# A fused Perceiver layer on one core: masks added to pairs of PSUM banks, the first key projection moved ahead of the scores, context loaded piece by piece

## The chip, the cores and the metric

The kernel runs on one core of a Trainium2 chip. The metric is the device time of one execution in microseconds (us), taken as the median of several runs. The engines named below are PE (matrix products), DVE and POOL (elementwise work), ACT (activations and copies), and SP, which here only issues DMA transfers. [...] Each engine works through its own instructions in the order in which they were written; engines meet through semaphores.

## The reference

The input is `x` (32 batches of 64 rows of 256) and a context of 1601 rows of 256 for each batch. Three blocks with residual connections follow each other. Cut to what matters here, the first is

```python
qh, kh, vh = split_heads(q @ wq + bq), split_heads(ctx @ wk + bk), split_heads(ctx @ wv + bv)
scores = einsum('bhqd,bhkd->bhqk', qh, kh) / sqrt(16)        # 16 heads of 16
attn   = softmax(where(mask, scores, -1e9), axis=-1)         # over 1601 keys
x      = x + merge(attn @ vh) @ wo + bo                      # q = layernorm(x)
```

The second block is attention over the 64 positions of a batch whose weights come from a learned mean and width for each position and head. The third is a feed-forward layer: a shared gated part and two of eight experts for each token, chosen by the token's number. All is float32.

## The kernel before, in words

The 1601 keys of a batch are padded to 13 blocks of 124. The context arrives transposed in four pieces for each batch (`GROUPS`: 4, 3, 3 and 3 blocks) through five buffers `ct` (`load_piece`, `load_context`). For each batch `project_keys(b, c, g)` makes the keys of one half `c` of the heads (eight heads) and one group `g`, and ACT copies them from PSUM to `kT` (L510). `project_values(b, u)` makes the values of two blocks and ACT copies them to `v` (L527). A projection is either one product over the whole array or "tiled", four products of 32 columns each (L495).

The attention of a half (b, c) is computed with keys on the partitions. `scores(n, g)` computes the blocks of one of three score groups (`SCORED`: 4, 5 and 4 blocks) for four pairs of heads, one pair to a bank; the fifth block of the middle group goes to an extra bank and to spare room beside the accumulators `pvs`. DVE adds the mask `madd` to each bank and writes the result to `prob` in SBUF (L573, for the fifth blocks L566), and keeps a running maximum over the blocks in `mrun` (L590). In what order DVE does this is written out by hand in the strings `ORDER`, `SOONER` and `LATER`: a digit is the mask of one bank, `m7` the maximum over block 7, `t` the maximum along rows, A and B the fifth blocks. PE turns the maxima (`pm`, L597), DVE reduces them along rows (L604), PE spreads them again (`pb`, L612), ACT copies them to `mb` (L616), POOL subtracts them from `prob` (L621), ACT takes the exponential (L626), and PE multiplies with the values (`pvs`, L636).

The main loop runs over 63 halves, n = 0 to 62. In the turn of half n the scores of half n+1 are computed, the softmax of half n is finished, the values of half n-1 are multiplied, and the next batch is projected. In a turn of before, PE's order is: values of n-1, place 0; first scores of n+1; `pm`; keys of group 0; `pb`; values of n-1, place 1; second scores; keys of group 1; two value projections; third scores; keys of groups 2 and 3, tiled; one or two value projections, tiled. Between them stand the steps of the second block for earlier tiles of 128 rows and of the queries for later ones (`span_steps`, `query_steps`), handed out by `agenda`: for a tile these are eleven products into PSUM (`tr_q`, `pq`, `po`, `tr_h`, `psp`, `pval`, `psa` twice, `po2`, `po3`, `tr_f`). The order on PE, DVE, ACT and POOL is the order of the program (`manual_schedule`).

The PSUM banks for all of this except `pvs` and `mrun` come from one pool of six tiles, `ps_x`, handed out in turn by `mm_bank`. Waits between engines are derived from the tiles that the instructions touch. Towards the end, units of the feed-forward layer (`unit`, `gate`, `linear_factor`) use the same six banks; the experts follow with pools of their own.

Of the kernel before, what the change touches and what calls it, by code (L numbers as in the profile page):

```python
# [23 lines left out]
P = 128  # L24
# [14 lines left out]
ORDER = [  # L39
    "0 1 t 2 3",  # L40
    "A 0 m3 1 B 2 m8 3 m4 m5",
    "0 1 m6 2 m7 3 m9 m10 m11 m12",
]
# [24 lines left out]

SOONER = "A 0 1 B 2 m8 3 m4 m5"
LATER = "A 0 m1 1 m2 B 2 m3 3 m8 m4 m5"  # L70

# [19 lines left out]
def perceiver_kernel(ctx: ExitStack, tc: tile.TileContext, a: dict[str, bass.AP], out: bass.AP):  # L91
# [9 lines left out]
    span_pool = ctx.enter_context(tc.tile_pool(name="span", bufs=1))  # L101
    ps_mm = None

# [3 lines left out]

    def mm_bank(name: str):
        return ps_mm.tile([P, 512], F32, tag="mm", name=name)

# [134 lines left out]
    def span_steps(t: int, oT):  # L245
# [148 lines left out]

    ps_x = xattn.enter_context(tc.tile_pool(name="ps_x", bufs=6, space=PSUM))
    ps_pv = xattn.enter_context(tc.tile_pool(name="ps_pv", bufs=1, space=PSUM))
    ps_m = xattn.enter_context(tc.tile_pool(name="ps_m", bufs=1, space=PSUM))
    ps_mm = ps_x


    madd = big.tile([P, NKC, S], F32, name="madd", bufs=1)
    nc.vector.tensor_scalar(madd[:CHUNK], m8[:CHUNK], -MASKED, MASKED, ALU.mult, ALU.add)
    nc.vector.tensor_scalar(
        madd[:CHUNK, NKC - 1, :], madd[:CHUNK, NKC - 1, :], cst[:CHUNK, C_PAD : C_PAD + 1],
        None, ALU.add,
    )

    madd_fifth = big.tile([P, P], F32, name="madd_fifth", bufs=1)
    for e in range(2):
        nc.gpsimd.tensor_copy(  # L410
            madd_fifth[:CHUNK, e * S : (e + 1) * S], madd[:CHUNK, SCORED[1][0] + 4, :]
        )

# [4 lines left out]
    def pair_of(n: int, j: int):  # L421
        return prob[:CHUNK, place(n, j // 2), j % 2]
# [59 lines left out]

    def load_context(b: int):
        for g in range(len(GROUPS)):
            load_piece(b, g)
        if b % 2 == 0 and b // 2 + 1 < NTILE:
            t = b // 2 + 1
            load_x(t)

# [42 lines left out]
    def scores(n: int, g: int, then=None, order=None):  # L532
# [5 lines left out]
        more = [mm_bank(f"psc_{b}_{c}_{g}"), spare_pvs] if nb == 5 else None  # L538
        pss = [mm_bank(f"psc_{b}_{c}_{g}_{j}") for j in range(4)]
        for r in range(nb):  # L540
# [17 lines left out]
        for item in (order or ORDER[g]).split():  # L558
            if item == "t":
                if held is not None:  # L560
                    maxima_of_rows(*held)
            elif item[0] == "m":
                maximum(n, int(item[1:]))
            elif item in "AB":
                k, e = c0 + 4, "AB".index(item)
                nc.vector.tensor_tensor(  # L566
                    block_of(n, k)[:, :, e, :],
                    more[e][:CHUNK, : 2 * P].rearrange("p (r q) -> p r q", r=2),
                    madd_fifth[:CHUNK, None, :].to_broadcast([CHUNK, 2, P]), ALU.add,
                )  # L570
            else:
                j = int(item)
                nc.vector.tensor_tensor(  # L573
                    pair_of(n, j)[:, c0 : c0 + 4, :].rearrange("p k (e q) -> p k e q", e=2),
                    pss[j][:CHUNK].rearrange("p (k e q) -> p k e q", k=4, e=2),
                    madd[:CHUNK, c0 : c0 + 4, None, :].to_broadcast([CHUNK, 4, 2, S]), ALU.add,
                )
# [81 lines left out]

    def half_unit(u: int, w):  # L660
        quarter, hc = divmod(u, NHC)
        slot = slice(quarter * QL, (quarter + 1) * QL)
        ps = mm_bank(f"u{u}")
        for c in range(2):
            nc.tensor.matmul(  # L665
                ps, lhsT=w[:, c, hc * P : (hc + 1) * P], rhs=xfT[:, c, :, slot],
                start=(c == 0), stop=(c == 1),
            )
        return ps.rearrange("p (r i) -> p r i", r=E)
# [8 lines left out]
    def unit(u: int):  # L678
        begun.append((u, half_unit(u, sw1), None if u in linear else half_unit(u, sw3)))

    def gate():
        u, p1, p3 = begun.popleft()
        quarter, hc = divmod(u, NHC)
        at = gated_at(quarter, hc)
# [77 lines left out]
    for u in range(7):  # L762
        project_values(0, u)
    last = len(halves) - 1

    extra = {3 * last - 3: (0,), 3 * last - 2: (1, 2, 4), 3 * last - 1: (5, 6)}
    for n, (b, c) in enumerate(halves[:-1]):
        if c == 0 and b + 1 < B:
            load_context(b + 1)
        if c and b % 2 == 0 and b // 2 + 1 < NTILE:  # L770
# [16 lines left out]
        if n:  # L787
            values(n - 1, 0)
            exponentials(n - 1, 3)
        scores(n + 1, 0, taken_off)  # L790
        project(project_keys, c, 0)
        m = maxima_along_rows(turned[1])
# [18 lines left out]
        exponentials(n, 0)  # L811
        project(project_keys, c, 1)
        for u in (4, 5) if c else (0, 1):
            project(project_values, u)
        less_maxima(n, 1, m, nc.gpsimd)
# [4 lines left out]
        scores(n + 1, 2)  # L820
        project(project_keys, c, 2, True)
        project(project_keys, c, 3, True)
        for u in (3, 6) if c else (2,):
            project(project_values, u, True)
# [179 lines left out]
```

## Time and profile before

| | before |
|---|---|
| median of 3 runs | 1520.34 us (1519.32 to 1524.4) |
| span of the profiled execution | 1515.7 us; its own time is not given apart, the runs lie 3.6 to 8.7 us above its span |
| granted PE clock, mean | 0.995 |
| PE busy | 1465.0 us, 97% |
| DVE busy | 1225.5 us, 81% |
| POOL busy | 1120.7 us, 74% |
| ACT busy | 946.9 us, 62% |

A group's row in the profile names the line, the engine, the operation, what it writes and reads with shapes and the number of instructions; then its busy time, the mean duration of one in ns, and the idle time of the engine just before such instructions with what ended most of it. Busy shares are means over the span. PE's ends are modelled, so that groups that follow each other overlap a little in the timeline.

### The profile page before, as it was taken

What the parts mean: (1) busy time and instruction counts of PE and PEld (TensorE: products, weight loads), DVE (VectorE), ACT (ScalarE), POOL (GpSimd) and SP (SyncE); (2) the same over time, 40 slices, a digit from 0 to 9 for tenths busy, and PEclk for the clock granted to TensorE, in tenths of its full rate; (3) what the DMA queues carried; (4) which work ended last, traced back from release to release, by engine and by line L of the source; (5) the groups of instructions that cost most, each with busy time, mean ns of one, the idle gap of its engine ahead of it and who ended that gap; (6) DMA issues with size and microseconds to landing.
All of it is one profiled execution on the core that took longest, in us unless ns stands there. A gap on an engine that the chain in (4) does not pass through costs nothing.

```text
span 1515.7 us, 62949 instructions
## 1 busy us (share of the span) xinstructions
PE 1465.0 (97%) x28600; PEld 1066.5 (70%) x28600; DVE 1225.5 (81%) x2332; ACT 946.9 (62%) x1727; POOL 1120.7 (74%) x508
## 2 busy tenths in 40 slices
PE   8999999999999999999999999999999999998899
PEld 5677767777777767777777777676777677654587
DVE  4889898998989898989989898988899898873100
ACT  3565657676767657576766677575767566766411
POOL 1777787888878887878888888878788788852710
PEclk9999999999999999999999999999999999999999
DMA  5111111111111101111111111011111111005200
GB/s 174 37 45 46 46 47 46 36 50 50 50 50 50 49 25 41 47 53 37 49 50 50 50 50 49 24 43 46 54 37 48 50 50 33 3 9 160 60 29 29
DMA packets 52076, 73.82 MB, mean 49 GB/s; under 512 B 3812, under 2 KB 51040, under 8 KB 51680
## 3 DMA queue, kind: packets, MB, share of 16 engines
q1 hardware_dynamic: 50992, 69.00, 14.9%
q8 instruction: 225, 3.69, 1.0%
q10 hardware_dynamic: 816, 0.79, 0.2%
q14 instruction: 43, 0.35, 0.1%
HBM read 65.57 MB, written 4.19 MB: 46 GB/s over the span
## 4 chain that ended last, share of the span: by engine, by line
PE 76%; DVE 17%; ACT 4%; issue 2%; POOL 0%; DMA 0%; ACTq 0%; DVEq 0%; POOLq 0%
PE pk L495 20%; PE pv L495 19%; PE psc L549 10%; PE pvs L636 10%; DVE mrun L590 8%; DVE prob L573 6%; PE py L934 4%; PE pm L597 2%; PE u L665 2%; PE ph L916 2%; PE pb L612 2%; ACT qbd L474 1%; PE psa L357 1%; PE pq L466 1%; PE po L377 1%
## 5 line engine op out<-in xcount | busy, mean ns | idle before, releaser
L621 POOL TENSOR_TENSOR prob<-prob,mb 124x1664 f32<-124x1664 f32 x252 | 939.0, 3751 | 224.2 <-ACT mb L616 218.8
L573 DVE TENSOR_TENSOR prob<-psc,madd 124x512 f32<-124x512 f32 x768 | 504.0, 680 | 76.5 <-PE psc L549 76.0
L626 ACT ACTIVATE prob<-prob 124x1664 f32<-124x1664 f32 x256 | 406.9, 1591 | 185.0 <-POOL prob L621 182.0
L590 DVE TENSOR_TENSOR mrun<-prob,mrun 124x512 f32<-124x512 f32 x704 | 486.7, 691 | 33.9 <-ACT mrun L582 20.1
L495 PE MATMUL pk<-ct,wkT_sb 128*32 128x372 f32 (+1 forms) x2512 | 387.6, 489 | 8.9 <-DMA wkT_sb<-in_wkT 5.5
L495 PE MATMUL pv<-wvT_sb,ct 128*124 128x256 f32 x3524 | 381.0, 379 | 0.9 <-DVE prob L566 0.8
L495 PEld LDWEIGHTS pv<-wvT_sb,ct 128*124 128x124 f32 x3524 | 272.8, 132 | 110.4 <-issue 17.5
L549 PE MATMUL psc<-qbd,kT 32*124 32x128 f32 x6400 | 241.8, 279 | 8.3 <-issue 6.9
L495 PEld LDWEIGHTS pk<-ct,wkT_sb 128*32 128x32 f32 (+1 forms) x2512 | 148.9, 127 | 140.1 <-issue 95.5
L549 PEld LDWEIGHTS psc<-qbd,kT 32*124 32x124 f32 x6400 | 201.9, 181 | 41.8 <-issue 20.8
L636 PE MATMUL pvs<-prob,v 124*17 124x64 f32 x13312 | 213.6, 220 | 3.0 <-issue 2.8
L527 ACT COPY v<-pv 124x512 f32<-124x512 f32 (+1 forms) x224 | 124.5, 556 | 146.5 <-PE pv L495 146.1
L636 PEld LDWEIGHTS pvs<-prob,v 124*17 124x17 f32 x13312 | 196.0, 98 | 27.9 <-issue 15.7
L510 ACT ACTIVATE kT<-pk,cols 128x372 f32<-128x372 f32 (+2 forms) x256 | 145.7, 585 | 70.0 <-PE pk L495 69.7
L323 ACT ACTIVATE sc<-sc,least 128x64 f32<-128x64 f32 x256 | 85.8, 343 | 2.6 <-DVE least L319 2.5
L936 DVE SCALAR_TENSOR_TENSOR ot<-py,prob 128x256 f32<-128x256 f32 x16 | 6.8, 424 | 75.7 <-PE py L934 66.1
L665 PE MATMUL u<-xfT,sw_sb 128*128 128x512 f32 x128 | 60.9, 624 | 3.6 <-ACT prob L692 2.7
L582 ACT COPY mrun<-prob 124x512 f32<-124x512 f32 x64 | 38.2, 596 | 37.3 <-DVE soft L306 34.3
L612 PEld LDWEIGHTS pb<-cst,mc 128*124 128x124 f32 x256 | 29.4, 135 | 36.6 <-DVE mc L604 30.0
L549 PE MATMUL pvs<-qbd,kT 32*124 32x128 f32 x256 | 54.9, 294 | 0.0
L597 PE MATMUL pm<-cst,mx 124*128 124x124 f32 x256 | 41.4, 283 | 11.4 <-DVE mx L590 10.1
L323 ACT ACTIVATION_READ_ACCUMULATOR sc<-sc,least 128x1 f32 x256 | 49.9, 195 | 0.0
(126 smaller groups left out, 1220.3 us busy)
## 6 DMA issues: line engine op xcount, KB each, us to landing
ct<-in_ctxT SPq DMA_DIRECT2D x64, 372.0 KB, 3.2
ct<-in_ctxT SPq DMA_DIRECT2D x32, 496.0 KB, 5.1
ct<-in_ctxT SPq DMA_DIRECT2D x32, 361.0 KB, 3.9
w<-in_w SPq DMA_DIRECT2D x16, 256.0 KB, 7.0
x<-in_x SPq DMA_DIRECT2D x16, 128.0 KB, 2.1
x_kept<-x SPq DMA_DIRECT2D x16, 128.0 KB, 2.0
prob<-x_kept SPq DMA_DIRECT2D x8, 256.0 KB, 6.3
out<-ot SPq DMA_DIRECT2D x16, 128.0 KB, 1.9
```

Source lines behind the costliest of these rows:

```text
L323: nc.scalar.activation(sc[:, h, :], sc[:, h, :], AF.Exp, bias=least[:, h : h + 1], scale=-1.0, accum_out=total[:, h : h + 1],)
L495: nc.tensor.matmul(out[at:end], lhsT=lhsT[:, at:end], rhs=rhs, start=start, stop=stop, **(dict(tile_position=(0, at)) if tiled else {}),)
L510: nc.scalar.activation(kTs[c][:, k0 : k0 + kn], ps[:, :kn], AF.Identity, bias=cols[:, B_K + c : B_K + c + 1])
L527: nc.scalar.copy(vs[b % 2][:kn, 2 * u : 2 * u + n, :, :DK], ps[:kn, : n * D].rearrange("p (n h d) -> p n h d", n=n, d=DK),)
L549: product = nc.tensor.matmul(ps[:CHUNK, at * P : (at + 1) * P], lhsT=kTs[c][32 * j : 32 * j + 32, k0 : k0 + CHUNK], rhs=qbd[b // 2][32 * j ...
L573: nc.vector.tensor_tensor(pair_of(n, j)[:, c0 : c0 + 4, :].rearrange("p k (e q) -> p k e q", e=2), pss[j][:CHUNK].rearrange("p (k e q) -> ...
L590: nc.vector.tensor_tensor(dst, block_of(n, k), run, ALU.max)
L597: nc.tensor.transpose(ps[:, j * CHUNK : (j + 1) * CHUNK], m[:CHUNK, j, :], ident[:CHUNK, :CHUNK])
L621: engine.tensor_tensor(sj, sj, m[:CHUNK, j, None, :].to_broadcast([CHUNK, NKC, P]), ALU.subtract)
L626: nc.scalar.activation(pair_of(n, j), pair_of(n, j), AF.Exp)
L636: nc.tensor.matmul(pvs[32 * j : 32 * j + DK + 1, c, :, r, :], lhsT=v[:kn, k, 8 * c + h, :], rhs=pair_of(n, h // 2)[:kn, k, (h % 2) * S : ( ...
L665: nc.tensor.matmul(ps, lhsT=w[:, c, hc * P : (hc + 1) * P], rhs=xfT[:, c, :, slot], start=(c == 0), stop=(c == 1),)
```

## The change

The six tiles of the pool become one tile `banks` of six banks, and `mm_bank` returns a slice of it; the bank is chosen by `take`, the one used longest ago. `mm_banks` takes two neighbouring banks, and the mask is then added to both by one instruction on 1024 columns; for this `madd` holds each column twice, and the strings of the order have two digits where they had four. Units of the feed-forward layer hold their banks until they are gated. In the main loop the keys of group 0 are projected, tiled, ahead of the first scores; the other projections are dealt out anew (group 2 is no longer tiled). The pieces of the context are no longer loaded together at the start of a batch's first half, but one by one, for the batch after the next, each behind the last reader of the buffer that it takes.

```diff
 ORDER = [
-    "0 1 t 2 3",
-    "A 0 m3 1 B 2 m8 3 m4 m5",
-    "0 1 m6 2 m7 3 m9 m10 m11 m12",
+    "0 t 1",
+    "A 0 m3 B 1 m8 m4 m5",
+    "0 m6 1 m7 m9 m10 m11 m12",
 ]
-SOONER = "A 0 1 B 2 m8 3 m4 m5"
-LATER = "A 0 m1 1 m2 B 2 m3 3 m8 m4 m5"
+SOONER = "A 0 B 1 m8 m4 m5"
+LATER = "A 0 m1 B 1 m2 m3 m8 m4 m5"
...
-    def mm_bank(name: str):
-        return ps_mm.tile([P, 512], F32, tag="mm", name=name)
+    NBANK = 6
+    taken = [0] * NBANK
+    held_banks: dict[str, int] = {}
+
+    def mm_bank(name: str, hold: bool = False):
+        i = take([[i] for i in range(NBANK)])[0]
+        if hold:
+            held_banks[name] = i
+        return banks[:, i, :]
+
+    def mm_banks(name: str):
+        i = take([[i, i + 1] for i in range(0, NBANK, 2)])[0]
+        return banks[:, i : i + 2, :]
+
+    def take(choices):
+        free = [c for c in choices if not set(c) & set(held_banks.values())]
+        best = min(free, key=lambda c: max(taken[i] for i in c))
+        for i in best:
+            taken[i] = max(taken) + 1
+        return best
...
-    ps_x = xattn.enter_context(tc.tile_pool(name="ps_x", bufs=6, space=PSUM))
+    ps_x = xattn.enter_context(tc.tile_pool(name="ps_x", bufs=1, space=PSUM))
...
-    ps_mm = ps_x
+    banks = ps_x.tile([P, NBANK, 512], F32, name="banks")
-    madd = big.tile([P, NKC, S], F32, name="madd", bufs=1)
-    nc.vector.tensor_scalar(madd[:CHUNK], m8[:CHUNK], -MASKED, MASKED, ALU.mult, ALU.add)
+    madd = big.tile([P, NKC, 2, S], F32, name="madd", bufs=1)
+    for e in range(2):
+        nc.vector.tensor_scalar(
+            madd[:CHUNK, :, e, :], m8[:CHUNK], -MASKED, MASKED, ALU.mult, ALU.add
+        )
...
-    madd_fifth = big.tile([P, P], F32, name="madd_fifth", bufs=1)
-    for e in range(2):
-        nc.gpsimd.tensor_copy(
-            madd_fifth[:CHUNK, e * S : (e + 1) * S], madd[:CHUNK, SCORED[1][0] + 4, :]
-        )
...
-    def load_context(b: int):
-        for g in range(len(GROUPS)):
+    def piece_ahead(b: int, g: int):
+        if b < B:
             load_piece(b, g)
-        if b % 2 == 0 and b // 2 + 1 < NTILE:
-            t = b // 2 + 1
-            load_x(t)
...
-        pss = [mm_bank(f"psc_{b}_{c}_{g}_{j}") for j in range(4)]
+        pairs = [mm_banks(f"psc_{b}_{c}_{g}_{i}") for i in range(2)]
+        pss = [pairs[j // 2][:, j % 2, :] for j in range(4)]
...
-                j = int(item)
+                i = int(item)
                 nc.vector.tensor_tensor(
-                    pair_of(n, j)[:, c0 : c0 + 4, :].rearrange("p k (e q) -> p k e q", e=2),
-                    pss[j][:CHUNK].rearrange("p (k e q) -> p k e q", k=4, e=2),
-                    madd[:CHUNK, c0 : c0 + 4, None, :].to_broadcast([CHUNK, 4, 2, S]), ALU.add,
+                    prob[:CHUNK, place(n, i), :, c0 : c0 + 4, :].rearrange(
+                        "p j k q -> p j (k q)"
+                    ),
+                    pairs[i][:CHUNK],
+                    madd[:CHUNK, None, c0 : c0 + 4].rearrange(
+                        "p j k e q -> p j (k e q)"
+                    ).to_broadcast([CHUNK, 2, 4 * P]),
+                    ALU.add,
                 )
...
     def unit(u: int):
-        begun.append((u, half_unit(u, sw1), None if u in linear else half_unit(u, sw3)))
+        first = half_unit(u, sw1, "a")
+        begun.append((u, first, None if u in linear else half_unit(u, sw3, "b")))
     def gate():
         u, p1, p3 = begun.popleft()
+        held_banks.pop(f"u{u}a")
+        held_banks.pop(f"u{u}b", None)
...
+    for g in range(len(GROUPS)):
+        load_piece(1, g)
...
     for n, (b, c) in enumerate(halves[:-1]):
-        if c == 0 and b + 1 < B:
-            load_context(b + 1)
+        if c == 0:
+            piece_ahead(b + 2, 0)
+            if b % 2 == 0 and b // 2 + 1 < NTILE:
+                load_x(b // 2 + 1)
...
+        project(project_keys, c, 0, True)
+        if c:
+            piece_ahead(b + 2, 1)
         scores(n + 1, 0, taken_off)
-        project(project_keys, c, 0)
+        if c:
+            project(project_values, 3)
+        else:
+            project(project_keys, c, 1)
...
         exponentials(n, 0)
-        project(project_keys, c, 1)
-        for u in (4, 5) if c else (0, 1):
-            project(project_values, u)
+        if c:
+            project(project_keys, c, 1)
+            piece_ahead(b + 2, 2)
+            project(project_values, 4)
+            project(project_keys, c, 2)
+            piece_ahead(b + 2, 3)
+        else:
+            project(project_keys, c, 2)
+            for u in (0, 1):
+                project(project_values, u)
...
         scores(n + 1, 2)
-        project(project_keys, c, 2, True)
         project(project_keys, c, 3, True)
-        for u in (3, 6) if c else (2,):
+        for u in (5, 6) if c else (2,):
             project(project_values, u, True)
```

## The prediction

> **What bounds the kernel now.** I read the page first (busy shares, clock row, costliest groups), then what PE waited for, then a stretch of the timeline in the steady state, then the granted clock around the few long idle stretches of PE. The page:
>
> ```profile
> span 1515.7 us, 62949 instructions
> ...
> PE 1465.0 (97%) x28600; PEld 1066.5 (70%) x28600; DVE 1225.5 (81%) x2332; ACT 946.9 (62%) x1727; POOL 1120.7 (74%) x508
> ...
> L573 DVE TENSOR_TENSOR prob<-psc,madd 124x512 f32<-124x512 f32 x768 | 504.0, 680 | 76.5 <-PE psc L549 76.0
> ...
> L626 ACT ACTIVATE prob<-prob 124x1664 f32<-124x1664 f32 x256 | 406.9, 1591 | 185.0 <-POOL prob L621 182.0
> ```
>
> Copies of ACT out of PSUM, with shapes kept apart:
>
> ```profile
> L527 ACT COPY v<-pv 124x512 f32<-124x512 f32 x192 | 112.6, 586 | 137.7 <-PE pv L495 137.2
> ...
> L510 ACT ACTIVATE kT<-pk,cols 128x372 f32<-128x372 f32 x128 | 71.4, 557 | 10.3 <-PE pk L495 10.2
> ```
>
> PE is busy 97% of the span; DVE, POOL and ACT have slack, and each waits for PE somewhere. In the waits of PE nothing steady is longer than this:
>
> ```profile
> PE pm L597 <- DVE mx L590: 10.1, 16, 2.4
> ...
> PE pb L612 <- DVE mc L604: 2.6, 3, 1.5
> ```
>
> So a faster DVE alone can win about 13 us. What keeps PE at 97% is seen in the timeline, PE first and ACT below (start, duration):
>
> ```profile
> 717.26 1.83 PE L495 MATMUL pk<-ct,wkT_sb 128*128 128x496 f32 x4
> 718.92 0.60 PE L612 MATMUL pb<-cst,mc 128*124 128x128 f32 x4
> 719.36 1.03 PE L251 MATMUL po<-woP_sb,oT 128*128 128x256 f32 x4
> ```
>
> ```profile
> 719.40 0.66 ACT L510 ACTIVATE kT<-pk,cols 128x496 f32<-128x496 f32 x1
> 719.96 0.58 ACT L616 COPY mb<-pb 124x512 f32<-124x512 f32 x1
> ```
>
> PE finishes the key bank, writes the next bank (pb) and is inside a third (po) before ACT even starts to empty the first. Six separately tracked banks let PE run ahead of ACT and DVE.
>
> **The change, step by step.**
>
> *One tile for six banks.* The pool of six tiles becomes one tile, `banks`, and every bank is a slice of it. In the built program of the changed kernel the waits follow the tile, not the bank. From the order of its instructions (batch 20, PE):
>
> ```
> L242 Matmult banks_137<-cst_64,xn_q10_11413 128x128 [waits Activation_49]
> L242 Matmult banks_137<-cst_64,xn_h8_11415 128x128 [waits Activation_49]
> L397 Matmult banks_137<-woutT_sb_104,o2T_6_10856 128x256 [waits Activation_49]
> ```
>
> Counting the increments of those semaphores, the first (bank 1) waits for the copy mb out of bank 0, the second (bank 2) for the copy xnT out of bank 1, the third (bank 3) for the copy hT out of bank 2. I followed four halves: each group of matmuls into any bank waits for the last read, in program order, of any other. So PE can no longer run ahead: matmul group, copy, matmul group, copy.
>
> Prices, from the timeline of before. From the point where PE could start its next group to the copy's start: 0.25 us on ACT (pk, v), 0.16 on DVE. Copies: 0.56 to 0.59 (pk, v), 0.67 (kT of 496 columns). End of read to PE's start: 0.05 to 0.1 (mc to pb). So an ACT copy that nothing hides costs 0.9 us, the one of 496 columns 1.0.
>
> *Masks in pairs.* The trace has no PSUM addition of 1024 columns. Bounds: 1.19 us (the DVE reduction of 128x1024 in the same trace, L319) and 1.36 (twice 680 ns). I take 1.21, by the slope from 691 ns at 512 to 1886 ns at 1664 on DVE (L590, L621). That takes 384 x 0.15 = 58 us of DVE work away, which would be worth the 13 us above and no more; but a wait on scores now lasts until both pairs are read. Back to back, starts are some 0.07 closer (0.60 against 0.68).
>
> Per half of a batch, in PE's order, the idle time that opens:
> - Tiled first keys, then first scores: the kT copy, 1.0, and it stands behind the exponential of place 3 on ACT (1.59): 1.35 in all.
> - First scores and pm, then keys or values: mask, row maxima, mask = 0.16+1.14+0.60+1.21+0.1 = 3.2.
> - That group, then pb: 0.9. The copy mb hides under the values matmuls (1.57).
> - Second scores, then keys: 0.16+0.34+1.14+0.34+1.21+0.1 = 3.3, plus 0.6 for a maximum between (m3, or the three before them): 3.9.
> - Three projections: 2.7. Third scores, then keys: mask, maximum, mask: 3.2.
> - Last keys 0.9; in every second half one more value group, 0.45 on the mean. The last copy hides under the values.
>
> Sum 16.6 us per half. A tile's steps (four halves) add eleven groups: copies exposed are mb three times (2.7), xnT and hT (1.4), qbd and psp (2.4), aT twice (1.8), the value copies ahead of pval and po2 (1.8), and about 3 where normalisations and small exponentials stand before the kT copy: 13, so 3.2 per half. With 19.8 us on 62 full halves: **+1228**. PE's own work per half is some 20.5 us, so a half goes from 20.7 to about 40.
>
> *Tiled keys moved.* Tiled projections run at 2.49 us per 733 columns, untiled at 1.36 per 372 and 1.67 per 496. Group 0 becomes tiled (1.69 for 1.67), group 2 untiled (1.36 for 1.26): +0.12 per half, +7, bounds 0 and 7. The moved group now lies between the last maximum and pm, which ends the pm wait; pb has other work before it. Both old waits go: -13. Nothing else is won, since the new waits stand on the same path.
>
> *Context by pieces.* Five buffers as before; a piece still waits for its buffer's last reader, and lands in 3.2 to 5.1 us, a half (20 us or more) ahead of use. On SP it passes the stores of x_kept and the x loads; PE's only DMA wait in the trace is the first weight. Zero; uncovered, one piece per half would cost 5. The wider madd costs one more DVE instruction (0.6) while DVE idles until 16.77 us, and two POOL copies go: zero.
>
> *Ends.* Before the first half: seven values and eight key copies at 0.9 and three scores at 3.3, less the waits there now: +22. After the last: about 16 round trips of gates (0.69+0.75+0.3), two tiles of steps, a half without projections: +58. Together +80.
>
> *Clock.* PE idle for three stretches of 3.2 to 3.9 us in each half is new. What idling does to the granted clock is in the trace near the end (stretch, length, PE busy, clock):
>
> ```profile
> 1344.77:1348.18 3.41, 0.98 (x40) 1.00 0.02 5
> 1348.18:1351.59 3.41, 2.64 (x64) 0.50 0.00 0
> 1351.59:1355.00 3.41, 3.41 (x60) 0.50 0.03 7
> ...
> 1399.38:1402.79 3.41, 1.39 (x4) 1.00 0.00 0
> 1402.79:1406.21 3.42, 0.00 (x0) 1.00 0.00 0
> 1406.21:1409.62 3.41, 3.21 (x40) 0.50 0.00 0
> ```
>
> The clock changes on a grid of 3.41 us. A stretch with PE busy 0.98 us (29%) halved it, one with 1.39 (41%) did not; one with 2.64 (77%) did not give it back, 3.21 (94%) did. With some 35% and 80%, a gap of 3.2 us leaves a low stretch in about 65 of 100 positions of the grid, one of 3.9 in 85. After the second scores PE's 4.9 us of work with gaps of 0.9 rarely fills a stretch: 3.5 us of doubled work expected; after the third 3.0 (5 us without a break follow); after the first 3.0. Less 1.5 that hides under the maxima and the exponential: 8 per half, **+496**. Bounds: nothing, and 18 (all 20.5 of PE's work doubled, less what hides).
>
> [...]
>
> [...]
>
> **Sum.** The profiled span is 1515.7 us, 4.6 under the median 1520.3. 1520 + 1228 + 7 - 13 + 80 + 496 = 3318; I say 3310.
>
> **The rivals.**
> - *One buffer, clock mostly up.* For: a gap of 0.9 (14.7 to 15.6 us in the trace) did not lower it. Against: the rows above. 1520+1228+74 = 2820.
> - *One buffer, clock low nearly throughout.* For: outside two unbroken runs per half nothing reaches 94%. 2820 + 62 x 18 = 3940.
> - *The banks stay independent on the chip* (other side). Then only the pairs and the move count: -13 for PE's two waits, 0 to +7 for the tiling, about 1510. It decides only if a bank's writer does not in fact wait for another bank's reader; the program's waits speak against it.
>
> **How the numbers follow.** Forecast 0.70, clock up 0.15, clock low 0.11, independent 0.04. The first alone: 2950 to 3650 (one us per half either way, clock 3 to 12). The range 2750 to 3700 takes in the second rival with one us per half less, and leaves out the other two. Faster by over 0.3% (the least that can be told from no change) 0.03, within 0.01, slower 0.96.
>
> **What would show it.** Right: PE busy falls to some 60% of the span or below; PE's waits are led by DVE prob and by the ACT copies (kT, v), thousands of times together instead of none; three PE gaps of 3 to 4 us per half; granted clock between 0.6 and 0.9; the pair addition near 1.2 us. Wrong: PE writing one bank before the other is read, or a clock of 1.0 with those gaps, or 0.5 throughout.

## The result, and the profile after

The changed kernel takes 3407.11 us (median of 4 runs, 3399.6 to 3411.3), the kernel before, run beside it, 1519.83 us (4 runs, 1516.25 to 1524.4). The ratio is 2.242, with a 95% interval of 2.235 to 2.249. Forecast were 3310 us, with a range of 2750 to 3700. The profiled execution took 3399.6 us; its span is 3397.8 us.

The page of the kernel after, the lines that answer to those shown of before:

```profile
span 3397.8 us, 62655 instructions
...
PE 2261.0 (67%) x28600; PEld 1372.0 (40%) x28600; DVE 1217.0 (36%) x1949; ACT 973.1 (29%) x1727; POOL 1109.3 (33%) x506
...
PEclk7667776677766767676776766777676676766779
...
L588 DVE TENSOR_TENSOR prob<-banks,madd 124x1024 f32<-124x1024 f32 x384 | 467.8, 1218 | 1273.1 <-PE banks L617 693.0
...
L646 ACT ACTIVATE prob<-prob 124x1664 f32<-124x1664 f32 x256 | 404.9, 1589 | 136.8 <-POOL prob L641 134.2
```

The 28600 products are the same number as before. DVE, ACT and POOL work about as long as before (1217.0, 973.1 and 1109.3 us for 1225.5, 946.9 and 1120.7), in a span more than twice as long. PE is idle for 1136.8 us (3397.8 less 2261.0), where it was 50.7. It is also busy for 796 us more with the same products: the row of the granted clock (PEclk, in tenths, 40 slices of the span) shows mostly 6 and 7, where the page of before has 9 throughout:

```profile
PEclk9999999999999999999999999999999999999999
```

So there are two losses, waits and clock.

The groups of ACT's copies out of PSUM, where PE writes its products, with shapes kept apart (after the bar: busy us, mean ns of one; then the idle time before them and its releaser):

```profile
L538 ACT COPY v<-banks 124x512 f32<-124x512 f32 x192 | 112.5, 586 | 817.2 <-PE banks L506 817.2
...
L521 ACT ACTIVATE kT<-banks,cols 128x372 f32<-128x372 f32 x128 | 73.0, 570 | 685.9 <-PE banks L506 685.9
```

The copies themselves are about as long as before (586 ns for 586, 570 for 557). But ACT now waits 817.2 us for PE ahead of the copies to `v` and 685.9 ahead of these copies to `kT`, where it waited 137.7 and 10.3.

What PE waited for in the kernel after (us in all, times, longest):

```profile
PE banks L506 <- DVE prob L588: 617.0, 189, 4.4
PE banks L561 <- ACT kT L521: 100.8, 81, 3.2
PE banks L506 <- ACT kT L521: 85.5, 127, 0.9
PE banks L506 <- ACT v L538: 68.6, 100, 0.7
```

L506 is a projection, L588 the mask on a pair of banks. No product of L506 reads what L588 writes. The projection writes another bank of the same tile, and it waits 189 times, three times per half, for the last mask.

The timeline of PE in the kernel after (start, duration; in brackets the idle time before and who ended it):

```profile
1525.94 1.15 PE L561 MATMUL banks<-qbd,kT 32*124 32x128 f32 x32 [3.21 <-ACT kT L521]
1527.02 0.64 PE L617 MATMUL banks<-cst,mx 124*128 124x124 f32 x4
1530.76 2.85 PE L506 MATMUL banks<-ct,wkT_sb 128*128 128x372 f32 x4 [3.10 <-DVE prob L588]
1534.27 1.11 PE L632 MATMUL banks<-cst,mc 128*124 128x128 f32 x4 [0.66 <-ACT kT L521]
1536.11 0.69 PE L242 MATMUL banks<-cst,xn_q 128*128 128x128 f32 x2 [0.73 <-ACT mb L636]
...
1546.95 1.59 PE L506 MATMUL banks<-ct,wkT_sb 128*128 128x372 f32 x4 [3.12 <-DVE prob L588]
1549.20 3.77 PE L506 MATMUL banks<-wvT_sb,ct 128*124 128x256 f32 x8 [0.66 <-ACT kT L521]
1553.65 3.77 PE L506 MATMUL banks<-wvT_sb,ct 128*124 128x256 f32 x8 [0.68 <-ACT v L538]
```

ACT in the same stretch:

```profile
1523.75 1.57 ACT L646 ACTIVATE prob<-prob 124x1664 f32<-124x1664 f32 x1
1525.23 0.65 ACT L521 ACTIVATE kT<-banks,cols 128x496 f32<-128x496 f32 x1
1533.65 0.57 ACT L521 ACTIVATE kT<-banks,cols 128x372 f32<-128x372 f32 x1 [7.76 <-PE banks L506]
1535.47 0.58 ACT L636 COPY mb<-banks 124x512 f32<-124x512 f32 x1 [1.26 <-PE banks L632]
```

Before, PE wrote the key bank, then pb, and was inside a third bank before ACT emptied the first. Now it is product, copy, product, copy: pb starts at 1534.27, after the key copy of 1533.65 has ended, and the next product starts after the copy of pb. The key copy at 1525.23 stands behind an exponential on ACT, and in this half behind small steps of the second block as well, and holds the first scores back by 3.21 us; that is the longest such wait. The projections of 1530 and 1549 take 2.85 and 3.77 us, nearly twice what the same shapes take at full clock (1.52 and 1.99 in the run with filled gaps below).

### The profile page after: what moved, and what is told of

The parts are those of the page before. It is cut to its first block, busy times and chain, and to the rows that moved or that the text cites. A ratio compares the mean times of both kernels' runs of the same rounds, so it can differ in the third digit from the quotient of the medians.

```text
span 3397.8 us, 62655 instructions
## 1 busy us (share of the span) xinstructions
PE 2261.0 (67%) x28600; PEld 1372.0 (40%) x28600; DVE 1217.0 (36%) x1949; ACT 973.1 (29%) x1727; POOL 1109.3 (33%) x506
## 4 chain that ended last, share of the span: by engine, by line
PE 61%; DVE 20%; ACT 17%; issue 2%; DMA 0%; DVEq 0%; SPq 0%; ACTq 0%
PE banks L506 36%; DVE prob L588 13%; PE banks L561 8%; PE pvs L656 5%; ACT kT L521 4%; ACT v L538 4%; ACT prob L646 4%; DVE mrun L610 2%; PE banks L685 2%; PE banks L632 2%; PE py L973 2%; DVE prob L578 1%; ACT sc L343 1%; PE banks L617 1%; DVE mc L624 1%
## 5 line engine op out<-in xcount | busy, mean ns | idle before, releaser
L506 PE MATMUL banks<-ct,wkT_sb 128*32 128x496 f32 (+1 forms) x2512 | 610.8, 707 | 552.4 <-DVE prob L588 520.6
L588 DVE TENSOR_TENSOR prob<-banks,madd 124x1024 f32<-124x1024 f32 x384 | 467.8, 1218 | 1273.1 <-PE banks L617 693.0
L506 PE MATMUL banks<-wvT_sb,ct 128*124 128x256 f32 x3524 | 680.6, 546 | 227.5 <-DVE prob L588 96.4
L506 PEld LDWEIGHTS banks<-wvT_sb,ct 128*124 128x124 f32 x3524 | 391.0, 192 | 567.9 <-ACT kT L521 222.4
L506 PEld LDWEIGHTS banks<-ct,wkT_sb 128*32 128x32 f32 (+1 forms) x2512 | 199.3, 164 | 766.9 <-DVE prob L588 557.4
L521 ACT ACTIVATE kT<-banks,cols 128x372 f32<-128x372 f32 (+2 forms) x256 | 151.7, 592 | 1079.4 <-PE banks L506 1079.1
L561 PE MATMUL banks<-qbd,kT 32*124 32x128 f32 x6400 | 294.5, 326 | 134.5 <-ACT kT L521 100.8
L538 ACT COPY v<-banks 124x512 f32<-124x512 f32 (+1 forms) x224 | 124.4, 556 | 857.0 <-PE banks L506 857.0
L561 PEld LDWEIGHTS banks<-qbd,kT 32*124 32x124 f32 x6400 | 252.1, 225 | 233.4 <-ACT kT L521 170.3
L685 PE MATMUL banks<-xfT,sw_sb 128*128 128x512 f32 x128 | 74.9, 736 | 34.8 <-DVE prob L716 20.4
L343 ACT ACTIVATE sc<-sc,least 128x64 f32<-128x64 f32 x256 | 85.4, 339 | 0.0
```

The lines of the kernel that those rows point to most:

```text
L343: nc.scalar.activation(sc[:, h, :], sc[:, h, :], AF.Exp, bias=least[:, h : h + 1], scale=-1.0, accum_out=total[:, h : h + 1],)
L506: nc.tensor.matmul(out[at:end], lhsT=lhsT[:, at:end], rhs=rhs, start=start, stop=stop, **(dict(tile_position=(0, at)) if tiled else {}),)
L521: nc.scalar.activation(kTs[c][:, k0 : k0 + kn], ps[:, :kn], AF.Identity, bias=cols[:, B_K + c : B_K + c + 1])
L538: nc.scalar.copy(vs[b % 2][:kn, 2 * u : 2 * u + n, :, :DK], ps[:kn, : n * D].rearrange("p (n h d) -> p n h d", n=n, d=DK),)
L561: product = nc.tensor.matmul(ps[:CHUNK, at * P : (at + 1) * P], lhsT=kTs[c][32 * j : 32 * j + 32, k0 : k0 + CHUNK], rhs=qbd[b // 2][32 * j ...
L588: nc.vector.tensor_tensor(prob[:CHUNK, place(n, i), :, c0 : c0 + 4, :].rearrange("p j k q -> p j (k q)"), pairs[i][:CHUNK], madd[:CHUNK, N ...
```

## The experiments

The kernel before was run beside each set: 1518.2 us for the first four runs, 1523.23 for the next four, 1518.17 for the last three. Ratios are to these.

### One tile alone

The kernel before, with its six banks as slices of one tile, handed out in turn. Nothing else of the change is in it: masks singly, projections and loads in their old places. In the last stretches a bank of the shared feed-forward part is handed out again before it is read, so part of that is not what the reference computes; the main loop is complete.

```diff
+    turn = [0]
+
     def mm_bank(name: str):
-        return ps_mm.tile([P, 512], F32, tag="mm", name=name)
+        turn[0] += 1
+        return banks[:, turn[0] % 6, :]
...
-    ps_x = xattn.enter_context(tc.tile_pool(name="ps_x", bufs=6, space=PSUM))
+    ps_x = xattn.enter_context(tc.tile_pool(name="ps_x", bufs=1, space=PSUM))
...
-    ps_mm = ps_x
+    banks = ps_x.tile([P, 6, 512], F32, name="banks")
```

> The kernel before with one edit: its six banks are six slices of one tile, handed out in the same turn. Masks bank by bank, projections and loads as before. If the waits by the whole tile are the cause: like the changed kernel, 3300 to 3650 us, about 3480 (four masks with maxima between them are read after each score group instead of two pairs, and one copy more stands open in each half), granted clock 0.65 to 0.8, PE's waits led by DVE prob. If the pairs of banks are the cause (two banks held until both are read, longer DVE instructions): 1515 to 1530. If the moved projections and loads are the cause: 1515 to 1530.

Measured: 3524.63 us, ratio 2.320 (2.302 to 2.339), granted clock 0.71. Its waits of PE:

```profile
PE banks L498 <- DVE prob L576: 724.4, 189, 5.1
PE banks L498 <- ACT kT L513: 128.4, 189, 0.8
```

These are the same 189 waits as in the kernel after, now behind four single masks instead of two pairs (L576 is the mask, L498 a projection): 3.83 us each instead of 3.26. So the tile alone gives more than the whole slowdown. Given one tile, the rest of the change wins some 118 us (3525 less 3407; the two runs of this kernel lie at 3501.9 and 3547.4, so the 118 is rough).

### Three tiles of two banks

The kernel after, with its six banks in three tiles.

```diff
-        return banks[:, i, :]
+        return banks[i // 2][:, i % 2, :]
...
-        return banks[:, i : i + 2, :]
+        return banks[i // 2]
...
-    banks = ps_x.tile([P, NBANK, 512], F32, name="banks")
+    banks = [ps_x.tile([P, 2, 512], F32, name=f"banks{i}") for i in range(NBANK // 2)]
```

> The changed kernel with one edit: the six banks are three tiles of two banks instead of one tile of six; the banks are chosen in the same way, masks in pairs and moves stay. If the whole tile is the cause: waits remain only between the two banks of a pair (pm and the next projection behind the first key copy and the row maxima, two value copies, the copy before the third scores), some 5 to 6 us per half in gaps under 2 us, which leave the clock up: 1700 to 2000 us, about 1860, clock over 0.95. If the pairs or the moves are the cause: above 3000, since both stay.

Measured: 2025.86 us, ratio 1.334 (1.328 to 1.339), clock 0.955. That is just outside the expected range. Nearly three quarters of the slowdown (3407 less 2026, of 3407 less 1520) go when PE can run ahead into another tile; what stays is led by waits of the same kind, a projection (L506) behind a copy or a reduction of another bank:

```profile
PE banks L506 <- ACT kT L521: 113.7, 126, 1.7
PE banks L506 <- DVE mc L624: 74.9, 62, 1.4
```

### The gaps filled

The kernel after with five banks in its tile, and in the sixth bank six idle products of 128x256 after each group of scores. They keep PE busy while it would wait, and nobody reads them. (Since five banks hold less, one unit of the feed-forward layer begins later, here and in the control below.)

```diff
+FILL = 6
...
-    NBANK = 6
+    NBANK = 5
...
+    idle = ps_x.tile([P, 512], F32, name="idle")
+
+    def fill(times: int):
+        for _ in range(times):
+            nc.tensor.matmul(idle[:, :D], lhsT=wkT[:, 0, :P], rhs=wvT[:, 0, :], start=True, stop=True)
...
         held = then() if then else None
+        fill(FILL)
...
```

> The changed kernel with five banks in its one tile instead of six (if writers wait for the whole tile anyway, that changes nothing) and six extra products of 128x256, whose result nobody reads, in a bank of their own after each score group, where PE waits 3 to 4 us for DVE; some 2.7 us at full clock. If the halved clock is a large part of the time: clock over 0.9, and the time falls although PE has more to do, to 2600 to 2900 us, about 2800 (the forecast without its clock term); the waits of PE for the ACT copies stay. If the clock is a mere sign and the waits alone make the time: 3400 or more, since the products only fill gaps or lengthen them.

Measured: 2828.85 us, ratio 1.862 (1.857 to 1.867), clock 0.954. More work, 578 us less time. In the timeline of PE, after the first scores (the profile counts twelve instructions for the six products), and below it the waits that are left behind the masks:

```profile
1507.40 2.76 PE L424 MATMUL idle<-wvT_sb,wkT_sb 128*128 128x256 f32 x12
1510.67 1.52 PE L513 MATMUL banks<-ct,wkT_sb 128*128 128x372 f32 x4 [0.50 <-DVE prob L599]
```

```profile
PE banks L513 <- DVE prob L599: 94.9, 154, 1.6
```

The filling ends 0.50 us before the mask lets the projection go, so it does not lengthen this wait; and the projection runs at full clock (1.52 us, not 2.85). In 154 of the 189 places a wait is left like this. In the other 35 the filling ended at the mask's end or after it; added up from the trace, it held those projections up by some 25 us in all.

### Five banks without the filling

The control for the run before: the same five banks, no idle products. The edit is against that run.

```diff
-FILL = 6
...
-    idle = ps_x.tile([P, 512], F32, name="idle")
-
-    def fill(times: int):
-        for _ in range(times):
-            nc.tensor.matmul(idle[:, :D], lhsT=wkT[:, 0, :P], rhs=wvT[:, 0, :], start=True, stop=True)
-
...
-        fill(FILL)
```

> The changed kernel with five banks in its one tile instead of six (the sixth bank is allocated and never written), so the same as the kernel of the run e4_filled but without its filling products. If each group of products waits for the last read of any bank of the tile, the number of banks is of no matter: 3390 to 3450 us, and what e4_filled won (2829) was the clock's alone. If a bank's own turn mattered too, one bank less would lengthen it by some copies of 0.9 us in each of 62 halves: 3460 or more; and then the comparison with e4_filled understates the clock.

Measured: 3417.8 us, ratio 2.245 (2.235 to 2.255), clock 0.705; the kernel after has 2.242 (2.235 to 2.249). The number of banks in the tile is of no matter. The filling wins 589 us against this control, and the clock goes from 0.705 to 0.954 with it, while PE's waits for the copies stay as they were (L571 or L564 on kT: 100.9 and 96.6 us; L513 or L506 on kT: 85.7 and 85.4). So what the filling wins is the clock's.

### The moves alone

The kernel before with its six tiles and single masks, and only the main loop's new order: tiled first keys ahead of the first scores, the later projections each one place earlier, the context by pieces.

```diff
             values(n - 1, 0)
             exponentials(n - 1, 3)
+        project(project_keys, c, 0, True)
+        if c:
+            piece_ahead(b + 2, 1)
         scores(n + 1, 0, taken_off)
-        project(project_keys, c, 0)
+        if c:
+            project(project_values, 3)
+        else:
+            project(project_keys, c, 1)
...
```

> The kernel before with only the moved work: keys of group 0 tiled ahead of the first scores, the other projections dealt out anew, context piece by piece. Six tiles and masks bank by bank as before. If the whole tile is the cause: 1500 to 1530 us; from the prediction's steps 1520 less up to 13 (the waits of pm and pb) plus up to 7 (tiling), so about 1514, PE's wait for the last maximum gone. If the moves are the cause: above 3000. If the pairs are the cause: as with the whole tile, so this run does not tell these two apart.

Measured: 1644.21 us, ratio 1.083 (1.080 to 1.086), clock 0.967. Expected was about 1514: a miss. Alone, the moves cost 126 us. The waits of PE name a copy:

```profile
PE pk L492 <- ACT kT L507: 48.3, 30, 2.6
PE pv L492 <- ACT kT L507: 38.6, 16, 2.8
```

The timeline, ACT first, then PE:

```profile
710.30 1.57 ACT L623 ACTIVATE prob<-prob 124x1664 f32<-124x1664 f32 x1
711.78 0.65 ACT L507 ACTIVATE kT<-pk,cols 128x496 f32<-128x496 f32 x1
```

```profile
709.98 0.64 PE L594 MATMUL pm<-cst,mx 124*128 124x124 f32 x4
712.48 1.63 PE L492 MATMUL pk<-ct,wkT_sb 128*128 128x372 f32 x4 [1.87 <-ACT kT L507]
713.91 1.06 PE L609 MATMUL pb<-cst,mc 128*124 128x128 f32 x4
```

Six banks are handed out in turn. With the first keys ahead of the four score banks and pm, the next projection is the seventh taker and gets the first keys' bank. Their copy stands on ACT behind the exponential of place 3, which here ran from 710.30. PE waits 1.87 us, and pb after the gap takes 1.06 us instead of 0.60. The granted clock of this run is 0.967, and 0.992 to 0.997 in the kernel before beside it: the clock went down as well. In the old order the first keys come after the first scores and pm, so the sixth taker after them is a step of another tile or the second scores, behind pb and the values, and by then the copy is done; the waits of PE in the kernel before name no copy to kT.

### The moves, with the keys ahead of the exponential

The kernel of the last run with two calls exchanged, which changes the order on ACT and not on PE.

```diff
             values(n - 1, 0)
-            exponentials(n - 1, 3)
         project(project_keys, c, 0, True)
+        if n:
+            exponentials(n - 1, 3)
```

> The kernel of e2_moves_only (1644 us) with one edit: in each half the tiled first keys are projected, and so copied by ACT, ahead of the exponential of place 3, not behind it. Theory (the copy kT stands on ACT behind an exponential that waits for POOL; six banks in turn hand the first keys' bank to the next projection, which waits for that copy, and the gap halves PE's clock): the 126 us go, 1515 to 1540 us, waits of pk and pv on kT near zero. Rival 1 (tiled products, or one projection more ahead of the scores, cost by themselves): 1600 to 1650. Rival 2 (the context by pieces costs it, its loads being late): 1600 to 1650, with waits of PE on the DMA.

Measured: 1524.14 us, ratio 1.0005 (0.9986 to 1.0024), clock 0.998. All 126 us are gone, so the cause is the copy's place on ACT, and neither the tiling nor the loads. What PE still waits for there, and ACT's order in its timeline:

```profile
PE pk L492 <- ACT kT L507: 17.1, 13, 1.4
...
PE pm L594 <- DVE mx L587: 5.8, 15, 2.4
```

```profile
699.91 0.68 ACT L507 ACTIVATE kT<-pk,cols 128x496 f32<-128x496 f32 x1 [1.38 <-PE pk L492]
700.48 1.58 ACT L623 ACTIVATE prob<-prob 124x1664 f32<-124x1664 f32 x1
```

### All parts, with separate tiles

The kernel after, but each pair of score banks is a tile of its own (two of them), and all else in the loop has two tiles of one bank in turn; after the loop there are six of one bank.

```diff
     def mm_banks(name: str):
-        i = take([[i, i + 1] for i in range(0, NBANK, 2)])[0]
-        return banks[:, i : i + 2, :]
+        return pools["two"].tile([P, 2, 512], F32, tag="two", name=name)
...
+    pools["one"] = ps_s.enter_context(tc.tile_pool(name="ps_one", bufs=2, space=PSUM))
+    pools["two"] = ps_s.enter_context(tc.tile_pool(name="ps_two", bufs=2, space=PSUM))
```

> All parts of the change as its edit reads, pairs, moved projections and pieces, but with the banks as separate tiles: two tiles of two banks for the pairs of scores, two tiles of one bank for all else in the loop (six of one bank after it). Theory (one tile for all six banks is what costs the 1890 us): most of it goes. What stays is what the moves alone cost (1644 us), and with only two banks for projections in turn somewhat more: the projection after the first scores, or the one after it, takes the bank of the first keys, whose copy stands on ACT behind the exponential of place 3. 1600 to 1800 us, I expect 1680. Rival (pairs and moves are themselves the cost, for instance because a mask of 1024 columns keeps four banks longer): over 2000, near the 2026 of three tiles.

Measured: 1651.57 us, ratio 1.084 (1.080 to 1.087), clock 0.981. The pairs and the moves as written, without the one tile, cost 128 us and not 1887.

### The pairs alone

The tiles of the last run, with the projections and loads of the kernel before.

```diff
-        project(project_keys, c, 0, True)
...
         scores(n + 1, 0, taken_off)
...
+        project(project_keys, c, 0)
...
```

> The kernel before with the pairs alone: the masks added to two banks by one instruction, the scores in two tiles of two banks, all else in the loop in two tiles of one bank; the order of the projections and the loads of the context as before. If pairs only take DVE's work away: DVE 50 us less busy, 1505 to 1520 us. If two banks in turn for the projections are too few: the second projection after the second scores takes the bank of the first one but one before it, whose copy stands behind the exponential of place 0 that waits for POOL, 1 to 2.5 us in each of 62 halves and a lower clock beside it: 1560 to 1720, I expect 1620. If the longer hold of the scores' banks were the cost, the waits would be those of psc on DVE prob.

Measured: 1606.63 us, ratio 1.056 (1.053 to 1.059), clock 0.991. DVE is busy for 1210.5 us, 15 us less than before, and not the 50 that were expected. The waits of PE on scores that are still being masked are 2.5 us in all; those on the key copies lead again:

```profile
PE pv L493 <- ACT kT L508: 26.0, 45, 1.9
PE tr_q L225 <- ACT kT L508: 15.0, 15, 1.1
```

By these waits it is not the longer hold of the scores' banks that costs, but that the pairs leave only two banks in turn for projections, maxima and steps, whose copies then come too late. The two waits shown are 41 of the 83 us, and no run keeps the pairs and changes the number of single banks, so this is argued and not shown.

### Separate tiles and the keys ahead of one exponential, then of three

First the run of all parts with the exchange of two calls shown above; then the same exchange for the exponentials of places 0 and 1; last that exchange in the kernel with six single banks.

```diff
+        if not c:
+            project(project_keys, c, 2)
+        else:
+            project(project_keys, c, 1)
         exponentials(n, 0)
         if c:
-            project(project_keys, c, 1)
...
         else:
-            project(project_keys, c, 2)
...
-        exponentials(n, 1)
         less_maxima(n, 2, m, nc.gpsimd)
         scores(n + 1, 2)
         project(project_keys, c, 3, True)
+        exponentials(n, 1)
```

> The kernel of e6_two_and_two (1652 us) with the edit of e7_moves_keys_before_exp: the first keys of each half ahead of the exponential of place 3. If the copy standing behind the exponential is most of what e6 loses, as it was all of what e2_moves_only lost: waits on kT fall from 74 us to some 20, the clock stays up, 1525 to 1570 us, I expect 1545; the two banks in turn leave more waits for copies than the six did. If two banks for the projections are too few in any order: 1600 or more. Faster than before only if the lighter DVE (50 us less) wins the 13 us of the old waits: 1505.

> The kernel of e9_two_and_two_keys_first with the same edit at the two other places of a half: a projection of keys goes ahead of the exponential of place 0 and one ahead of that of place 1, so that no copy of a key bank stands behind an exponential that waits for POOL. If e9 still loses to copies behind exponentials: 10 to 30 us below e9, so 1510 to 1540. If what is left there comes from the two banks, or from exponentials that are late for the weighted sums: no faster than e9, or slower.

> The kernel of e7_moves_keys_before_exp (1524 us; six banks, masks singly) with the edit of e10 at the two other places. Its PE waits are 17 us on kT, 5.8 on the last maximum and 4.6 on the turned maxima; the first would go: 1505 to 1515 us, so a little below before. If they turn into waits of the weighted sums for late exponentials: 1520 to 1535.

Measured: 1575.52 us for the first (ratio 1.037, 1.035 to 1.040), just above its range; 1567.13 for the second (1.0315, 1.029 to 1.034), where 1510 to 1540 were expected; 1528.49 for the third (1.006, 1.0045 to 1.008). The waits of PE in the second and then in the third, on the key copies and on the exponentials:

```profile
PE pk L490 <- ACT kT L505: 8.8, 14, 0.9
...
PE pvs L640 <- ACT prob L630: 5.7, 17, 0.3
```

```profile
PE pk L492 <- ACT kT L507: 14.7, 13, 1.4
PE pvs L633 <- ACT prob L623: 6.8, 18, 1.1
```

The exchange wins 71 us of the 128 (57 over before are left). Two more exchanges win 8, and with six banks they lose some 9 (1.006 against 1.0005): the exponentials come late for the weighted sums (pvs), whose wait was 0.6 us in all in the kernel with one exchange and whose products are busy for 202.1 us instead of 197.4. What the second still loses to the kernel before (49 us) is settled only in part. Its clock is 0.998, and PE is both more idle (70 against 51 us) and longer busy (1491 against 1465) than before. By the groups with shapes kept apart, some 31 us of this lie at the second block's steps (`tr_q`, `tr_h`, `tr_f`, `po`, `psp`, `psa`, `pval`): they are busy for 105 us instead of 95 and have 29 us idle ahead of them instead of 8; the idle time that was added stands mostly behind copies of ACT (v, kT, xnT). These steps follow each other through the two single banks, so two banks in turn are the likely cause; no run tests it, and the rest is open. No version that was tried is faster than the kernel before.

## Why the prediction was right

**The mechanism.** It was that every group of products into any bank waits for the last read of any other bank. The single edit that makes one tile gives 2.32 times the time; taking the tile apart gives 1.08. The rival in which the banks stay independent is out for the kernel as built. With separate tiles PE does run ahead, so the stop is put there by the waits that are derived from the tile. The built program waits by tile, and the measured price of that is 2006 us with the rest as before (3524.63 less 1518.2), or some 1755 with the rest as in the change (3407.11 less 1651.57).

**The waits: 1302 us forecast** (1228 for the halves, 80 for the ends, 7 less 13 for the moves). The kernel with filled gaps, at a clock of 0.954, lies 1311 us above before (2828.85 less 1518.2). I added up PE's busy time in its stretches at half clock: 236 us. The projection that took 2.85 us in the kernel after takes 1.52 at full clock, so at most half of the 236 would go, an estimate, and the waits by themselves are worth 1193 to 1311 us; the 25 us by which the filling itself came late may lower this a little further. The forecast is inside, at the upper end. Its terms were read off from the point where PE could start its next group, and the profile's idle time begins at the modelled end of a product, which lies up to 0.17 us later (in the timeline of before, a projection ends at 719.09 and pb starts at 718.92). The wait of a projection for the masks was put at 3.2, 3.9 and 3.2 us, 3.43 on the mean; the idle time is 617.0 us in 189 waits, 3.26. By place it is 3.10, 3.57 and 3.13, so only the middle one was put too high. A copy that nothing hides was put at 0.9 us; the idle time is 0.66 to 0.73, so 0.83 to 0.90 with the overlap. The first scores' wait for the key copy was put at 1.35; in the trace 63 of the 81 waits of scores for a key copy stand behind the tiled first keys, 88.9 us in all or 1.41 on the mean.

**The clock: 496 us forecast,** with bounds of nothing and 18 us per half. The filled gaps win 578 us against the kernel after and 589 against their control, and at most 118 more would come with the rest of the clock: 578 to 707, or 9.3 to 11.4 us per half where 8 were forecast. This is the term of the sum that was mis-sized, by 82 us or more; with the waits about at their forecast or below, it accounts for the 97 us between 3310 and 3407. If the waits are at the lower end of what was measured, the two errors partly cancel, and the closeness of the sum is in that part luck. The step that failed is the bound for halving, put at "some 35%" between two rows of before (29% busy halved the clock, 41% did not). In the kernel after, too, the clock changes on a grid of 3.4133 us. Stretches of that grid (length, PE busy, then granted clock, third from the end):

```profile
1503.88:1507.29 3.41, 2.09 (x24) 1.25 (x28) 0.00 (x0) 1.78 (x7) 1.88 (x1) 1.00 0.06 8
1507.29:1510.71 3.42, 0.58 (x24) 0.39 (x16) 2.70 (x3) 2.17 (x6) 0.00 (x0) 1.00 0.32 101
1510.71:1514.12 3.41, 2.64 (x16) 0.59 (x16) 3.27 (x6) 0.40 (x1) 0.00 (x0) 0.50 0.00 0
1514.12:1517.53 3.41, 3.20 (x32) 1.34 (x32) 0.35 (x1) 0.16 (x1) 0.00 (x0) 0.50 0.02 5
1517.53:1520.95 3.42, 2.70 (x131) 2.03 (x128) 0.00 (x0) 1.86 (x3) 0.00 (x0) 1.00 0.09 10
1520.95:1524.36 3.41, 1.78 (x24) 0.30 (x13) 0.00 (x0) 3.41 (x12) 0.00 (x0) 1.00 0.42 143
1524.36:1527.77 3.41, 1.73 (x36) 1.37 (x36) 0.00 (x0) 1.52 (x2) 0.00 (x0) 1.00 0.00 0
1527.77:1531.19 3.42, 0.43 (x1) 0.43 (x2) 2.94 (x3) 0.00 (x0) 0.00 (x0) 0.50 0.00 0
```

In this trace, each stretch's clock nearly always follows from the busy share of the one before. Over 880 such stretches in a row (from 91 to 3094 us), sorted by that share: at full clock, all 114 with less than 45% were followed by half clock; of 42 between 45 and 55%, 31 were; of 185 above 55%, one was. At half clock, none of 206 below 79% was followed by full clock, 48 of 233 between 79 and 85%, 33 of 35 between 85 and 90%, and all 65 above. So the bound for halving lies near half in this trace, not at a third. By the prediction's own reckoning, a gap of 3.2 us then leaves a low stretch in about 94 of 100 positions of the grid, not in 65. The bound for getting the clock back (80% forecast) was nearly right. The one row of before that kept its clock at 41% has no counterpart here and stays unexplained. That the bound makes up the whole of what the clock term lacked was not tested apart.

In the stretches shown above, halvings follow stretches that were 17% (0.58 us) and 51% (1.73 us) busy. That a stretch need not be wholly idle, as the forecast took from the row with 0.98 us busy, holds here too; but that row did not lead far enough.

**The pairs.** The mask of 1024 columns was put at 1.21 us; it took 1.218. The forecast that this takes 58 us of DVE work away was wrong: 504.0 became 467.8, 36 us, since single masks of 680 ns overlap with their neighbours (504.0 by 768 is 656 ns for each). DVE's whole busy time fell by 8.5 us only (1225.5 to 1217.0), because single masks overlap with the maxima between them too (in the timeline of DVE before, a mask of 0.68 us starts at 691.30 and the maximum after it at 691.90). In the run with the pairs alone the 13 us were not won either: with only two banks in turn left beside them they cost 83 (1606.63 less 1523.23).

**The moves.** "Both old waits go: -13", and the 7 added for the tiling, cannot be judged by the sum, in which they are lost among larger terms. Alone they cost 126 us. The forecast had seen that the key copy stands behind the exponential, and priced it in the one-tile kernel; it overlooked that with separate banks in turn the next projection waits for the same copy. So the price of the rival with independent banks, 1510, was off by some 140 us: in the one arrangement that was built, two pairs and two single banks, it is 1652. With the two calls exchanged the moves are worth +0.05%, -0.14 to +0.24, and the pm wait went from 10.1 to 5.8 us only. Loads by pieces cost nothing: in that kernel PE's one wait for a DMA is the first weight (5.4 us), as before (5.5).

**What would show it.** Waits led by DVE prob and the copies, three gaps of 3 to 4 us per half, and a clock between 0.6 and 0.9 (0.708) are there. "Thousands of times" is not: the four leading waits come to 497 times, all waits of PE together to 803. PE's busy share is 67% and not 60% or below, because the loss to the clock shows as busy time: the same 28600 products are busy for 2261.0 us instead of 1465.0, and a projection at half clock for 2.85 us where it takes 1.52 at full clock.

## What to carry to other kernels

Before joining buffers into one tile for the sake of a wider instruction, look in the built program for what each writer then waits for: where waits follow the tile, a ring of six banks becomes a ring of one, and that made this kernel take 2.3 times as long. A projection that is moved ahead takes with it its copy's place in ACT's queue and its place in the turn of banks; exchanging two calls on ACT was worth 126 us. PE was the bound here, and its gaps of 3 us were paid twice, once as waiting (1136.8 us idle instead of 50.7) and once in the clock (0.708 instead of 0.995), so that useless work in them shortened the time, from 3418 to 2829 us.

## What was not expected of the hardware

- Idle products made the kernel faster: with 2304 more instructions on PE it went from 3418 to 2829 us, by the clock (0.705 to 0.954).
- In the kernel after, the clock went down on its grid of 3.4133 us after stretches that were less than about half busy (all 114 below 45%, 31 of 42 between 45 and 55%, one of 185 above), and came back after those that were more than about 85% busy (98 of 100; 48 of 233 between 79 and 85%). The two bounds lie far apart, so that at half clock PE could be three quarters busy without getting its clock back (of 112 stretches between 60 and 79%, none was followed by full clock; the longest time at half clock from 91 to 3094 us is 30.7 us).
